# Layer 0's projections and router products in 32-column pieces, and the FFN's first weight tile moved by 224 bytes

## The chip, the cores and the metric

The kernel runs on one core of a Trainium2 chip. The metric is the device time of one execution in microseconds; of several runs the median is taken. A core has five engines that run side by side, each through its own instructions in order: TensorE (PE in the profile) multiplies, and its weight loads have a row of their own (PEld); VectorE (DVE), ScalarE (ACT) and GpSimd (POOL) work elementwise; SyncE (SP) issues most DMAs. Products land in PSUM, and everything else lies in SBUF, 128 partitions wide.

## The reference

Two transformer layers with post-norm on x of shape (8, 512, 512), all in float32:

```python
x = layernorm(x + attn0(x))   # 16 heads of 32, causal, with biases on Q, K, V and O
x = layernorm(x + moe(x))     # 8 experts, top 2, a router with a low-rank addition
x = layernorm(x + attn1(x))   # RMS-scaled input, 8 query heads of 64, 2 key heads
x = layernorm(x + ffn(x))     # gate, up and down from integers: (w - 128) * scale, width 1408
```

The router takes the softmax of the logits of each token, keeps the two largest, and divides them by their sum. An expert is silu(gate) * up and a down projection, with a low-rank addition to each weight.

## The kernel before

**Stages.** `usual_pass` runs four stages, one after the other on TensorE: attention of layer 0 with the routing (`attention0`, to about 712 us), the experts over tiles of 128 gathered tokens (`Tiles`), attention of layer 1 (`Attention1`, from about 1127 us), and the integer FFN (`IntegerFfn`, from about 1677 us). A batch is 512 tokens, held as four tiles of 128 rows; D = 512 is four chunks of 128. A float32 matmul of the program appears in the trace as two weight loads and two matmuls.

**A slot of layer 0.** For each batch b (8), each group g of four heads (4) and each unit u of key tiles (3), `attention0` issues one slot: `scores(b, g, u)` (L1386; keys of 32 rows, so four heads side by side in row groups of the array, 32\*128 in the profile), then the thunks that `plan(b)` put into this slot, then the `product` of the slot before (L1410; values of 32 columns, four heads side by side in column groups, 128\*32). Where a group ends, `normalise` follows (L1425, also 128\*32).

The thunks are the rest of the layer: `value`, `query` and `key` of this batch or the next (L1294, L1301, L1313), `project`, the output projection of the batch before (L1321), and the router two batches behind: `choose` (its gathers at L503 turn the four partial logits into eight per token), `dispatch` (ranks, L547 and L548), and `enter` (tables of tokens by expert, L588, in bf16). All these use the whole array, 128\*128. Others are `score` (logits, L491, 128\*32), `turn` (transposes, 128\*128) and `merge` (L781, 16 rows in a row group). In batches 1 to 6 each slot but the last of its twelve holds one or two projections.

Each projection is four products of 128 x 128 by 128 x 512, summed in one of two PSUM buffers (`p_mm`), and is taken out by VectorE (v, q, x) or ScalarE (k, and q of one group). The output projection of the last batch, the tables of the last two, and the gathers and ranks of the last run after the heads' buffers are closed, among the first expert tiles.

**What sets the order.** The framework orders each engine's instructions from dependences, the order of writing and its own estimate of durations. In the stretches under `in_order` (the first slot, and from the third group of the last batch on) TensorE follows the written order by force; in between the trace shows it in that order too. Other engines' orders are planned there.

**The FFN's weights.** `IntegerWeights` keeps the 33 units of 512 columns in two tiles. The first, `ffn_w0` of 20 units, is opened before layer 1's attention in the pool `c_weights` at the right end of SBUF; it holds the gate and up weights of hidden chunks 0 to 9. The second holds the down weights and chunk 10. `hidden` multiplies 128-column slices of them, as the stationary operand, with the two halves (high and low) of x (L1152 in the profile), 16 products a chunk; the down products (L1168) have the hidden tile as stationary operand and the weights as moving one.

**Layer 1** already makes most of its projections from two products of 64 columns each (`Attention1.multiply`, L1600).

Of the kernel before, what the change touches and what calls it, by code (L numbers as in the profile page):

```python
# [9 lines left out]
F32 = mybir.dt.float32  # L10
# [8 lines left out]
P = 128  # L19
# [3 lines left out]
NT = S // P  # L23
ND = D // P
E = 8
# [27 lines left out]

V_BQ, V_BK, V_NS, V_SS, V_SG, V_SU = 0, 4, 8, 12, 16, 16 + NHID
N_VEC = 16 + 2 * NHID


def in_order(tc, *engines):
# [358 lines left out]
class Router:  # L417
# [73 lines left out]
            self.nc.tensor.matmul(ps[32 * c : 32 * (c + 1), :], lhsT=self.wr[:, c, :], rhs=x1T[:, c, :],  # L491
                                  start=True, stop=True)

    def choose(self, b, parts, ps):

        nc, small = self.nc, self.small
        here = slice(NT * b, NT * (b + 1))

        def bc(a):
            return a[:, :, None].to_broadcast([P, NT, E])  # L500

        for t in range(NT):
            nc.tensor.matmul(ps[:, t, :], lhsT=parts[:, ts(t, P)], rhs=self.gather, start=True, stop=True)  # L503
        pr = small.tile([P, NT, E], F32, name="pr")
        tmp = small.tile([P, NT, E], F32, name="tmp")
        top = small.tile([P, NT], F32, name="top")
        second = small.tile([P, NT], F32, name="second")
        red = small.tile([P, NT], F32, name="red")
        total = small.tile([P, NT], F32, name="total")
        nc.vector.tensor_reduce(red, ps, AX.X, ALU.max)  # L510
        nc.vector.tensor_tensor(tmp, ps, bc(red), ALU.subtract)
        nc.scalar.activation(tmp, tmp, AF.Exp)
        nc.vector.tensor_reduce(red, tmp, AX.X, ALU.add)
        nc.vector.reciprocal(red, red)
        nc.vector.tensor_tensor(pr, tmp, bc(red), ALU.mult)

        def first_of_largest(values, largest, one_hot):
            nc.vector.tensor_reduce(largest, values, AX.X, ALU.max)
            nc.vector.tensor_tensor(tmp, values, bc(largest), ALU.is_equal)
            nc.vector.tensor_tensor(tmp, tmp, self.iota, ALU.mult)  # L520
            nc.vector.tensor_reduce(red, tmp, AX.X, ALU.min)
            nc.vector.tensor_tensor(one_hot, self.iota, bc(red), ALU.is_equal)

        first_of_largest(pr, top, self.hots[:, 0, here, :])

        rest = small.tile([P, NT, E], F32, name="rest")
        nc.vector.scalar_tensor_tensor(rest, self.hots[:, 0, here, :], -2.0, pr, ALU.mult, ALU.add)
        first_of_largest(rest, second, self.hots[:, 1, here, :])
        nc.vector.tensor_tensor(total, top, second, ALU.add)
        nc.vector.reciprocal(total, total)  # L530
        nc.vector.tensor_tensor(self.weights[:, 0, here], top, total, ALU.mult)
        nc.vector.tensor_tensor(self.weights[:, 1, here], second, total, ALU.mult)


        self.both = small.tile([P, NT, E], F32, name="both")
        nc.vector.tensor_tensor(self.both, self.hots[:, 0, here, :], self.hots[:, 1, here, :], ALU.add)
        self.earlier = small.tile([P, NT, E], F32, name="earlier")
        nc.vector.tensor_copy(self.earlier[:, 0, :], self.carry)
        for t in range(1, NT):
            nc.vector.tensor_tensor(self.earlier[:, t, :], self.earlier[:, t - 1, :], self.both[:, t - 1, :], ALU.add)  # L540
        nc.vector.tensor_tensor(self.carry, self.earlier[:, NT - 1, :], self.both[:, NT - 1, :], ALU.add)

    def dispatch(self, b, ps):

        nc, small = self.nc, self.small
        flat = "p t e -> p (t e)"
        nc.tensor.matmul(ps.rearrange(flat), lhsT=self.before, rhs=self.both.rearrange(flat), start=True, stop=False)  # L547
        nc.tensor.matmul(ps.rearrange(flat), lhsT=self.ones, rhs=self.earlier.rearrange(flat), start=False, stop=True)  # L548
        here = slice(NT * b, NT * (b + 1))
        parts = small.tile([P, TOP_K, NT], F32, name="parts")  # L550
        for k in range(TOP_K):
            for of_expert, out in ((ps, self.ranks[:, k, here]), (self.part, parts[:, k, :])):
                mine = small.tile([P, NT, E], F32, name="mine")
                nc.vector.tensor_tensor(mine, of_expert, self.hots[:, k, here, :], ALU.mult)
                nc.vector.tensor_reduce(out, mine, AX.X, ALU.add)

        rank = small.tile([P, TOP_K, NT], I32, name="rank")
        nc.vector.tensor_copy(rank, self.ranks[:, :, here])
        tile_of = small.tile([P, TOP_K, NT], I32, name="tile_of")
        nc.vector.tensor_scalar(tile_of, rank, 7, None, ALU.arith_shift_right)  # L560
        nc.vector.tensor_scalar(rank, rank, P - 1, None, ALU.bitwise_and)
        self.to_lane = small.tile([P, TOP_K, NT], F32, name="to_lane")
        nc.vector.tensor_copy(self.to_lane, rank)
        nc.vector.tensor_tensor(self.to_column[:, :, here], tile_of, parts, ALU.add)
# [15 lines left out]
                                    ALU.is_equal)  # L580
        return low, high, column

    def enter(self, ps, low, high, column):

        nc, n = self.nc, TOP_K * NT
        for h, part in enumerate((low, high)):
            for i in range(n):
                nc.tensor.matmul(ps[:, h, :], lhsT=part[:, i, :], rhs=column[:, i, :], start=i == 0, stop=i == n - 1)  # L588
        nc.vector.tensor_tensor(self.table, ps[:, 0, :], self.table, ALU.add)
        nc.vector.scalar_tensor_tensor(self.table, ps[:, 1, :], float(P), self.table, ALU.mult, ALU.add)  # L590

# [631 lines left out]
def attention0(env, guard, keep, routes, experts, dram, p_mm, tiles_ctx):  # L1223
# [8 lines left out]
    with ExitStack() as phase:  # L1232
# [55 lines left out]
        def mm(shape, name):  # L1288
            return p_mm.tile(shape, F32, tag="mm", name=name)

        def value(b, t):
            ps = mm([P, D], "ps_v")
            for c in range(ND):
                nc.tensor.matmul(ps, lhsT=xts[b][:, c, ts(t, P)], rhs=wv[:, c, :], start=c == 0, stop=c == ND - 1)  # L1294
            vs[t] = own.tile([P, D], F32, tag=f"v{t}", name=f"v{t}")
            nc.vector.tensor_tensor(vs[t], ps, row[:, 0, :], ALU.add)

        def query(b, g):
            ps = mm([P, S], "ps_q")
            for c in range(ND):  # L1300
                nc.tensor.matmul(ps, lhsT=wq[:, g, ts(c, P)], rhs=xts[b][:, c, :], start=c == 0, stop=c == ND - 1)  # L1301
            q = own.tile([P, S], F32, tag="q", name="q", bufs=2)
            if g == ND - 1 and 0 < b <= by_blocks:

# [5 lines left out]
        def key(b, g):  # L1310
            ps = mm([P, S], "ps_k")
            for c in range(ND):
                nc.tensor.matmul(ps, lhsT=wk[:, g, ts(c, P)], rhs=xts[b][:, c, :], start=c == 0, stop=c == ND - 1)  # L1313
            k = own.tile([P, S], F32, tag="k", name="k", bufs=2)
            nc.scalar.activation(k, ps, AF.Identity, bias=vec[:, V_BK + g : V_BK + g + 1])
            heads[b, g].append(k)

        def project(b, t):
            ps = mm([P, D], "ps_o")
            for c in range(ND):  # L1320
                nc.tensor.matmul(ps, lhsT=aoTs[b][:, c, ts(t, P)], rhs=wo[:, c, :], start=c == 0, stop=c == ND - 1)  # L1321
            nc.vector.tensor_tensor(xs[b][:, t, :], ps, xs[b][:, t, :], ALU.add)
            if t == NT - 1:
                env.layernorm(b, router.rows[S * b : S * (b + 1)])
# [34 lines left out]
            else:  # L1359
                nc.scalar.copy(logits[b], ps)  # L1360

        def choose(b):
            router.choose(b, logits.pop(b), mm([P, NT, E], "ps_r"))

        def dispatch(b, mm=mm):
            router.dispatch(b, mm([P, NT, E], "ps_rank"))

        rooms = {}

# [2 lines left out]
                rooms[b] = work.tile([P, ND, S], F32, tag="x1T", name="one_hot")  # L1372
            return router.one_hot(b, rooms[b], places)

        def enter(rows, mm=mm):
            router.enter(mm([P, 2, E * E_TILES], "ps_table"), *rows)

        def scores(b, g, u):
            q, k = heads[b, g]
# [162 lines left out]
        tiles.step(merge)  # L1542
        b = NB - 1
        one_hot(b - 1, (0, 1))
        project(b, 0)
        project(b, 1)
        rows = one_hot(b - 1, (2, 3))
        project(b, 2)
        project(b, 3)
        experts.load(7)  # L1550
        enter(rows)
        for _ in range(2):
            tiles.step()
            merge()
# [2 lines left out]
        tiles.step()  # L1557
        score(b)
        merge()
        choose(b)  # L1560
        tiles.step()
        merge()
        dispatch(b, tiles.aside)
        for places in ((0, 1), (2, 3)):
            rows = one_hot(b, places)
            tiles.step()
            merge()
        enter(rows, tiles.aside)
        tiles.of_fixed = router.fixed(routes)
        while merges:  # L1570
            tiles.step()
# [5 lines left out]
class Attention1:  # L1577
# [17 lines left out]
        return self.p_mm.tile(shape, F32, tag="mm", name=name)  # L1595

    def multiply(self, b, out, lhsT, rhs, c):

        for m in (slice(0, self.HD), slice(self.HD, P)) if b else (slice(0, P),):
            self.nc.tensor.matmul(out[m], lhsT=lhsT[:, m], rhs=rhs, start=c == 0, stop=c == ND - 1)  # L1600

    def prepare(self, b):

# [264 lines left out]
def usual_pass(tc, ins, held_out):  # L1868
    nc = tc.nc
    with ExitStack() as ctx:  # L1870
# [4 lines left out]
        with tc.tile_pool(name="a_mm", bufs=2, space=PSUM) as p_mm, ExitStack() as attn1_ctx:  # L1875
# [26 lines left out]
            for b in range(2, NB):  # L1902
                load_rows(b)
            weights = IntegerWeights(env, guard)
            weights.open(ctx.enter_context(tc.tile_pool(name="c_weights", bufs=1, side="right")), weights.FIRST)
            ffn = IntegerFfn(env, guard, weights, rows, dram)
            last_norm = attention.run(weights, ffn.split)
        ffn.run(held_out, last_norm)
# [306 lines left out]
```

## Time and profile before

| | |
|---|---|
| median of 3 runs | 2182.87 us (2181.64 to 2183.12) |
| the profiled execution: time | 2183.3 us |
| its span in the profile | 2181.6 us |
| TensorE busy, matmuls | 2151.6 us, 99% of the span, 9694 of them |
| V, Q, K, O projections of layer 0, busy | 116.3, 120.7, 117.5, 115.9 us |
| gathers, ranks, tables (all batches), busy | 7.7, 5.6, 15.3 us |
| FFN: gate and up, busy by four groups | 139.0, 138.8, 138.7, 138.6 us |

A row of the timeline gives a start, a length, engine, line, operation, the tile written and those read, rows\*columns of the array that the matmul uses, the moving operand's shape, and how many instructions were merged. Matmuls overlap:[...] lengths add up to more than the time taken, and the difference of two ends is the better measure. Busy time counts overlapping rows of a group once.

### The profile page before, as it was taken

The page shows a single profiled execution, that of the slowest core. Times are in us where ns is not written, and L with a number is a line of the kernel's source. Part 1 is how long each engine was busy: PE and PEld are TensorE (multiplying, and loading weights), DVE is VectorE, ACT ScalarE, POOL GpSimd, SP SyncE. Part 2 cuts the span into 40 slices and gives each one's busy share as a digit, 9 for nine tenths or more (in the row PEclk, how much of TensorE's full clock was granted, in tenths as well). Part 3 has the DMA queues.
Part 4 walks back from the last instruction along what each step waited for, and adds up shares of the span by engine and source line. Part 5 has one row for each costly group of instructions (what it writes and reads, how often), then busy time and mean ns, then how long its engine had stood idle before and what let it go on. Part 6 is the DMA issues. An engine that isn't in the chain of part 4 may idle for free. (4 is left out here: it accounts for less than half of the span.)

```text
span 2181.6 us, 25149 instructions
## 1 busy us (share of the span) xinstructions
PE 2151.6 (99%) x9694; PEld 1077.7 (49%) x9694; DVE 1273.8 (58%) x2042; ACT 627.5 (29%) x907; POOL 497.8 (23%) x489
## 2 busy tenths in 40 slices
PE   9999999999999999999999999999999999999997
PEld 3334444444444444444443333333334888888876
DVE  3557665675758543324316988889857644555443
ACT  2332323323223231122123333333332232222222
POOL 2332414324233442132015122231211000000000
PEclk9999999999999999999999999999999999999999
DMA  8030302303132328787644121331201311111000
GB/s 304 20 94 4 97 20 78 97 1 97 33 102 78 107 67 232 212 228 207 192 142 157 49 87 58 97 97 39 78 1 44 102 59 58 58 58 58 20 20 21
DMA packets 159971, 194.87 MB, mean 89 GB/s; under 512 B 61011, under 2 KB 101971, under 8 KB 157283
## 3 DMA queue, kind: packets, MB, share of 16 engines
q1 hardware_dynamic: 148560, 157.49, 23.5%
q0 software_dynamic: 10560, 34.61, 5.5%
q8 instruction: 79, 1.29, 0.2%
q10 hardware_dynamic: 722, 1.07, 0.1%
q14 instruction: 50, 0.40, 0.1%
HBM read 123.67 MB, written 69.47 MB: 89 GB/s over the span
## 5 line engine op out<-in xcount | busy, mean ns | idle before, releaser
L903 PE MATMUL ps_gu<-experts,xrT 128*128 128x512 f32 (+1 forms) x520 | 247.2, 598 | 0.0
L1390 ACT ACTIVATE p<-sc 128x2048 f32<-128x2048 f32 (+1 forms) x96 | 152.9, 1592 | 162.2 <-PE sc L1386 135.8
L1157 DVE SCALAR_TENSOR_TENSOR hT<-ps_u,vec,sg 128x512 f32<-128x512 f32 x88 | 65.6, 745 | 194.6 <-PE ps_u L1152 194.6
L1395 POOL TENSOR_SCALAR_AFFINE_SELECT p<-p 128x512 f32<-128x512 f32 x128 | 92.4, 734 | 360.3 <-ACT p L1390 316.8
L1168 PE MATMUL ps_f<-ffn_w,h_half 128*128 128x512 f32 x672 | 170.3, 393 | 0.6 <-issue 0.4
L1007 POOL TENSOR_TENSOR g_total<-g_total,r_inv 128x512 f32<-128x512 f32 x64 | 89.6, 1400 | 343.7 <-DVE r_inv L1778 272.2
L1418 DVE TENSOR_TENSOR p<-p 128x1536 f32<-128x1536 f32 (+2 forms) x96 | 131.1, 1365 | 46.0 <-POOL p L1395 41.0
L1748 ACT ACTIVATE p<-sc 128x1024 f32<-128x1024 f32 x128 | 124.0, 1021 | 100.4 <-PE sc L1745 95.9
L905 DVE TENSOR_TENSOR h<-ps_gu,h 128x256 f32<-128x256 f32 x67 | 28.4, 424 | 208.8 <-ACT h L904 208.8
L1778 DVE RECIPROCAL r_inv<-r_inv 128x512 f32<-128x512 f32 x32 | 107.1, 3346 | 69.3 <-ACT r_inv L1004 69.3
L1168 PEld LDWEIGHTS ps_f<-ffn_w,h_half 128*128 128x128 f32 x672 | 124.3, 188 | 33.1 <-DVE h_half L1163 5.6
L903 PEld LDWEIGHTS ps_gu<-experts,xrT 128*128 128x128 f32 x520 | 95.8, 196 | 89.3 <-issue 89.0
L1152 PE MATMUL ps_g<-x_high,ffn_w 128*128 128x512 f32 x352 | 138.8, 394 | 0.9 <-DVE x L1719 0.9
L1152 PE MATMUL ps_g<-x_low,ffn_w 128*128 128x512 f32 x352 | 139.0, 395 | 0.0
L1152 PE MATMUL ps_u<-x_low,ffn_w 128*128 128x512 f32 x352 | 138.7, 394 | 0.0
L1152 PE MATMUL ps_u<-x_high,ffn_w 128*128 128x512 f32 x352 | 138.6, 394 | 0.0
L919 PE MATMUL ps_y<-experts,hT 128*128 128x512 f32 (+1 forms) x272 | 128.0, 593 | 0.5 <-ACT hT L913 0.5
L1745 PE MATMUL sc<-qT,kT 64*128 64x512 f32 x512 | 127.2, 615 | 1.0 <-ACT qT L1653 0.7
L1301 PE MATMUL ps_q<-experts 128*128 128x512 f32 x256 | 120.7, 613 | 4.8 <-DMA experts<-in_xT 4.5
L1767 PE MATMUL av<-p,v 128*64 128x512 f32 x512 | 120.9, 593 | 0.0
L1313 PE MATMUL ps_k<-experts 128*128 128x512 f32 x256 | 117.5, 602 | 0.0
L1600 PE MATMUL ps_o<-attn_out,aoT 128*64 128x512 f32 x512 | 116.4, 598 | 0.8 <-ACT r_inv L1004 0.8
(267 smaller groups left out, 3359.6 us busy)
## 6 DMA issues: line engine op xcount, KB each, us to landing
results<-y SPq DMA_DIRECT2D x68, 256.0 KB, 2.2
turned<-turned SPq DMA_DIRECT2D x56, 256.0 KB, 4.1
pair<-xrT SPq DMA_DIRECT2D x25, 512.0 KB, 2.9
xrT<-pair SPq DMA_DIRECT2D x100, 128.0 KB, 4.3
x<-in_x SPq DMA_DIRECT2D x8, 1024.0 KB, 8.5
experts<-in_gate_up SPq DMA_DIRECT2D x8, 1024.0 KB, 11.0
rows<-x SPq DMA_DIRECT2D x32, 256.0 KB, 2.3
x<-rows SPq DMA_DIRECT2D x8, 1024.0 KB, 16.2
```

The lines of the kernel that those rows point to most:

```text
L903: nc.tensor.matmul(ps, lhsT=xT[:, c, :], rhs=self.weights(i, c), start=c == 0, stop=c == ND - 1)
L919: self.nc.tensor.matmul(ps, lhsT=hT[:, c, :], rhs=self.weights(i, ND + c), start=c == 0, stop=c == self.NI - 1)
L1152: nc.tensor.matmul(ps, lhsT=w[:, ts(dc, P)], rhs=x[:, dc, :], start=(dc, i) == (0, 0), stop=(dc, i) == (ND - 1, 1))
L1168: self.nc.tensor.matmul(os[t], lhsT=h[:, ts(t, P)], rhs=self.weights(2 * NHID + c), start=(c, i) == (0, 0), stop=(c, i) == (NHID - 1, 1))
L1301: nc.tensor.matmul(ps, lhsT=wq[:, g, ts(c, P)], rhs=xts[b][:, c, :], start=c == 0, stop=c == ND - 1)
L1313: nc.tensor.matmul(ps, lhsT=wk[:, g, ts(c, P)], rhs=xts[b][:, c, :], start=c == 0, stop=c == ND - 1)
L1390: nc.scalar.activation(p, sc[:, :, :width], AF.Exp, scale=scale)
L1418: nc.vector.tensor_tensor(total[:, :, P * kt :], total[:, :, P * kt :], p[:, :, at : at + w], ALU.add)
L1600: self.nc.tensor.matmul(out[m], lhsT=lhsT[:, m], rhs=rhs, start=c == 0, stop=c == ND - 1)
L1745: nc.tensor.matmul(sc[:, j, :], lhsT=st["kT"][hs, ts(kt, P)], rhs=st["qT"][g][hs, :], start=True, stop=True)
L1748: nc.scalar.activation(p, sc, AF.Exp, scale=scale)
L1767: nc.tensor.matmul(st["av"][HD * j : HD * (j + 1), :], lhsT=st["v"][:, kt, HD * j : HD * (j + 1)], rhs=p[:, j, :], start=kt == 0, stop=kt ...
```

## The change

A helper, `matmul_by_columns`, writes one product as several, each with 32 columns of the stationary operand into 32 partitions of the output. Layer 0's value, query, key and output projections use it, and so do the router's gathers, ranks and tables, as long as they run among the heads; after the heads' buffers are closed, the products keep their 128 columns (`out_of_heads`, `columns=P`). `Attention1.multiply` calls the helper with the widths that it had. Beside that, the pool of the FFN's first weight tile gets a second tile of 56 float32 (224 bytes) that nothing reads or writes.

```diff
+def matmul_by_columns(nc, out, lhsT, rhs, start=True, stop=True, columns=32):
+    for at in range(0, P, columns):
+        m = slice(at, at + columns)
+        nc.tensor.matmul(out[m], lhsT=lhsT[:, m], rhs=rhs, start=start, stop=stop)
...
-            nc.tensor.matmul(ps[:, t, :], lhsT=parts[:, ts(t, P)], rhs=self.gather, start=True, stop=True)
+            matmul_by_columns(nc, ps[:, t, :], parts[:, ts(t, P)], self.gather, columns=columns)
...
-        nc.tensor.matmul(ps.rearrange(flat), lhsT=self.before, rhs=self.both.rearrange(flat), start=True, stop=False)
-        nc.tensor.matmul(ps.rearrange(flat), lhsT=self.ones, rhs=self.earlier.rearrange(flat), start=False, stop=True)
+        out = ps.rearrange(flat)
+        matmul_by_columns(nc, out, self.before, self.both.rearrange(flat), stop=False, columns=columns)
+        matmul_by_columns(nc, out, self.ones, self.earlier.rearrange(flat), start=False, columns=columns)
...
-                nc.tensor.matmul(ps[:, h, :], lhsT=part[:, i, :], rhs=column[:, i, :], start=i == 0, stop=i == n - 1)
+                matmul_by_columns(nc, ps[:, h, :], part[:, i, :], column[:, i, :], i == 0, i == n - 1, columns)
...
+        def multiply(out, lhsT, rhs, c):
+            matmul_by_columns(nc, out, lhsT, rhs, start=c == 0, stop=c == ND - 1)
...
-                nc.tensor.matmul(ps, lhsT=wq[:, g, ts(c, P)], rhs=xts[b][:, c, :], start=c == 0, stop=c == ND - 1)
+                multiply(ps, wq[:, g, ts(c, P)], xts[b][:, c, :], c)
...
+        def wide(out, lhsT, rhs, c):
+            nc.tensor.matmul(out, lhsT=lhsT, rhs=rhs, start=c == 0, stop=c == ND - 1)
+
+        def project(b, t, out_of_heads=False):
...
+                (wide if out_of_heads else multiply)(ps, aoTs[b][:, c, ts(t, P)], wo[:, c, :], c)
...
-        def choose(b):
-            router.choose(b, logits.pop(b), mm([P, NT, E], "ps_r"))
+        def choose(b, columns=HD):
+            router.choose(b, logits.pop(b), mm([P, NT, E], "ps_r"), columns)
...
-        project(b, 0)
-        project(b, 1)
+        project(b, 0, True)
+        project(b, 1, True)
...
-        enter(rows)
+        enter(rows, columns=P)
...
-            weights.open(ctx.enter_context(tc.tile_pool(name="c_weights", bufs=1, side="right")), weights.FIRST)
+            pool = ctx.enter_context(tc.tile_pool(name="c_weights", bufs=1, side="right"))
+            weights.open(pool, weights.FIRST)
+            pool.tile([P, 56], F32, name="c_aligned")
```

`value` and `key` change as `query` does, and `dispatch` takes `columns` as `choose` does. `HD` is 32 in `attention0`, `P` is 128.

More of the change, by code (lines that the diff above doesn't have):

```diff
@@ L492, in logits, with choose @@
                                   start=True, stop=True)
-    def choose(self, b, parts, ps):
+    def choose(self, b, parts, ps, columns):
         nc, small = self.nc, self.small
@@ L541, in choose, with dispatch @@
         nc.vector.tensor_tensor(self.carry, self.earlier[:, NT - 1, :], self.both[:, NT - 1, :], ALU.add)
-    def dispatch(self, b, ps):
+    def dispatch(self, b, ps, columns):
         nc, small = self.nc, self.small
         flat = "p t e -> p (t e)"
-        nc.tensor.matmul(ps.rearrange(flat), lhsT=self.before, rhs=self.both.rearrange(flat), start=True, stop=False)
-        nc.tensor.matmul(ps.rearrange(flat), lhsT=self.ones, rhs=self.earlier.rearrange(flat), start=False, stop=True)
+        out = ps.rearrange(flat)
+        matmul_by_columns(nc, out, self.before, self.both.rearrange(flat), stop=False, columns=columns)
+        matmul_by_columns(nc, out, self.ones, self.earlier.rearrange(flat), start=False, columns=columns)
         here = slice(NT * b, NT * (b + 1))
@@ L581, in one_hot, with enter @@
         return low, high, column
-    def enter(self, ps, low, high, column):
+    def enter(self, ps, low, high, column, columns):
         nc, n = self.nc, TOP_K * NT
@@ L1293, in value @@
             for c in range(ND):
-                nc.tensor.matmul(ps, lhsT=xts[b][:, c, ts(t, P)], rhs=wv[:, c, :], start=c == 0, stop=c == ND - 1)
+                multiply(ps, xts[b][:, c, ts(t, P)], wv[:, c, :], c)
             vs[t] = own.tile([P, D], F32, tag=f"v{t}", name=f"v{t}")
@@ L1312, in key @@
             for c in range(ND):
-                nc.tensor.matmul(ps, lhsT=wk[:, g, ts(c, P)], rhs=xts[b][:, c, :], start=c == 0, stop=c == ND - 1)
+                multiply(ps, wk[:, g, ts(c, P)], xts[b][:, c, :], c)
             k = own.tile([P, S], F32, tag="k", name="k", bufs=2)
@@ L1316, in key @@
             heads[b, g].append(k)
-        def project(b, t):
+        def wide(out, lhsT, rhs, c):
+            nc.tensor.matmul(out, lhsT=lhsT, rhs=rhs, start=c == 0, stop=c == ND - 1)
+        def project(b, t, out_of_heads=False):
             ps = mm([P, D], "ps_o")
             for c in range(ND):
-                nc.tensor.matmul(ps, lhsT=aoTs[b][:, c, ts(t, P)], rhs=wo[:, c, :], start=c == 0, stop=c == ND - 1)
+                (wide if out_of_heads else multiply)(ps, aoTs[b][:, c, ts(t, P)], wo[:, c, :], c)
             nc.vector.tensor_tensor(xs[b][:, t, :], ps, xs[b][:, t, :], ALU.add)
@@ L1360, in score, with dispatch @@
                 nc.scalar.copy(logits[b], ps)
-        def choose(b):
-            router.choose(b, logits.pop(b), mm([P, NT, E], "ps_r"))
-        def dispatch(b, mm=mm):
-            router.dispatch(b, mm([P, NT, E], "ps_rank"))
+        def choose(b, columns=HD):
+            router.choose(b, logits.pop(b), mm([P, NT, E], "ps_r"), columns)
+        def dispatch(b, mm=mm, columns=HD):
+            router.dispatch(b, mm([P, NT, E], "ps_rank"), columns)
         rooms = {}
@@ L1373, in one_hot, with enter @@
             return router.one_hot(b, rooms[b], places)
-        def enter(rows, mm=mm):
-            router.enter(mm([P, 2, E * E_TILES], "ps_table"), *rows)
+        def enter(rows, mm=mm, columns=HD):
+            router.enter(mm([P, 2, E * E_TILES], "ps_table"), *rows, columns)
         def scores(b, g, u):
@@ L1544, in attention0 @@
         one_hot(b - 1, (0, 1))
-        project(b, 0)
-        project(b, 1)
+        project(b, 0, True)
+        project(b, 1, True)
         rows = one_hot(b - 1, (2, 3))
-        project(b, 2)
-        project(b, 3)
+        project(b, 2, True)
+        project(b, 3, True)
         experts.load(7)
-        enter(rows)
+        enter(rows, columns=P)
         for _ in range(2):
@@ L1559, in attention0 @@
         merge()
-        choose(b)
+        choose(b, P)
         tiles.step()
         merge()
-        dispatch(b, tiles.aside)
+        dispatch(b, tiles.aside, P)
         for places in ((0, 1), (2, 3)):
@@ L1567, in attention0 @@
             merge()
-        enter(rows, tiles.aside)
+        enter(rows, tiles.aside, P)
         tiles.of_fixed = router.fixed(routes)
@@ L1597, in multiply @@
     def multiply(self, b, out, lhsT, rhs, c):
-        for m in (slice(0, self.HD), slice(self.HD, P)) if b else (slice(0, P),):
-            self.nc.tensor.matmul(out[m], lhsT=lhsT[:, m], rhs=rhs, start=c == 0, stop=c == ND - 1)
+        matmul_by_columns(self.nc, out, lhsT, rhs, c == 0, c == ND - 1, self.HD if b else P)
     def prepare(self, b):
```

## The prediction

> **What bounds the kernel.** I read the page's first part, then busy time by stretch, then the waits of TensorE, then single stretches of the timeline.
>
> ```profile
> PE 2151.6 (99%) x9694; PEld 1077.7 (49%) x9694; DVE 1273.8 (58%) x2042; ACT 627.5 (29%) x907; POOL 497.8 (23%) x489
> core 0: us, PE busy (x) PEld busy (x) DVE busy (x) ACT busy (x) POOL busy (x), PEclk, DMA share, GB/s
> 14.00:697.00 683.00, 677.34 (x3526) 284.11 (x3530) 430.99 (x757) 213.44 (x232) 227.13 (x205) 1.00 0.24 76
> ...
> 1677.00:2170.00 493.00, 491.99 (x2114) 394.19 (x2114) 243.19 (x407) 130.49 (x205) 10.37 (x18) 1.00 0.16 53
> PE sc L1386 <- ACT p L1390: 2.0, 2, 1.8
> PE rs L1425 <- DVE first_h L905: 1.8, 1, 1.8
> PE ps_logits L491 <- ACT scaled L792: 1.7, 6, 0.3
> ```
>
> TensorE works through all four stages; the change touches the first (layer 0's attention, to 712 us) and the last (the integer FFN, from 1677 us). In the first it waits for others some 8 us from 14 us on, half of that after 690 us, in the last batch. So time that TensorE itself doesn't need is time gained, and the question is what TensorE's 677 us hold besides streaming.[...] One slot and a stretch of an earlier batch:
>
> ```profile
> 299.31 1.45 PE L1321 MATMUL ps_o<-experts,aoT 128*128 128x512 f32 x3
> 300.69 1.06 PE L1410 MATMUL av<-p,v 128*32 128x512 f32 x8
> 301.57 1.04 PE L1425 MATMUL rs<-p,ones 128*32 128x512 f32 x8
> 302.54 0.71 PE L1386 MATMUL sc<-q,k 32*128 32x256 f32 x8
> 303.19 3.70 PE L1313 MATMUL ps_k<-experts 128*128 128x512 f32 x8
> 306.72 3.60 PE L1321 MATMUL ps_o<-experts,aoT 128*128 128x512 f32 x8
> 310.16 1.91 PE L588 MATMUL ps_table<-one_hot 128*128 128x256 bf16 x16
> ...
> 55.14 1.14 PE L1386 MATMUL sc<-q,k 32*128 32x512 f32 x8
> 56.21 0.64 PE L1410 MATMUL av<-p,v 128*32 128x256 f32 x8
> ```
>
> A float32 product is two records. L1321's eight end 3.43 us after L1313's eight: 0.429 us a record. L1425's eight, four 32-column products side by side, end 0.86 us after L1410's: twice 0.429, so four narrow products cost what one 128-column product costs. The rest shows where the shape changes. L1313 ends at 306.89, 3.64 after L1386's end (303.25), 0.21 over eight times 0.429. L1410 at 300.69 ends 0.99 after L1321, 0.13 over 0.86. L1386 ends 0.64 after L1425, 0.21 over the 0.43 of two rows of 256. The last two lines are the change that the edit would leave: L1386 ends at 56.28, L1410 at 56.85, 0.57, which is 0.14 over 0.43.
>
> Over all single records from 14 to 712 us, by median, with the number of changes: rows (32\*128) to full (128\*128) 220 ns, 86; full to columns (128\*32) 121 ns, 78; rows to columns 120 ns, 18; columns to rows 215 ns, 91; full to rows 196 ns, 13; columns to full 220 ns, 5. Inside one shape the excess is 2 ns. (0.13 and 0.14 above hold 0.02 of stagger among four pieces.)
>
> In the FFN:
>
> ```profile
> 1911.05 0.39 PE L1152 MATMUL ps_g<-x_high,ffn_w 128*128 128x512 f32 x1
> ...
> 1914.77 1.98 PE L1168 MATMUL ps_f<-ffn_w,h_half 128*128 128x512 f32 x8
> 1916.59 0.39 PE L1152 MATMUL ps_g<-x_high,ffn_w 128*128 128x512 f32 x1
> ...
> 1920.21 1.98 PE L1168 MATMUL ps_f<-ffn_w,h_half 128*128 128x512 f32 x8
> ```
>
> These are hidden chunks 9 and 10 of a batch, 16 products each: 3.72 us and 3.62 us. By single records, products whose stationary operand lies in the first weight tile (chunks 0 to 9) start 233.2 ns apart in the mean, all others in the stage (chunk 10 from the second tile, and the down products, whose stationary operand is the hidden tile) 226.7. The program's addresses: the first tile begins at byte 138720 of a partition, 32 past a multiple of 64; the second at 92416, a multiple of 256; the hidden tiles are multiples of 256 too.
>
> [...] no run here shows a narrow bf16 load. [...] on entering a shape, the second float32 load starts 107 ns after the first at 128 columns and 27 ns after four staggered ones at 32. [...] the 6.5 ns rest on the trace alone.
>
> **The change part by part.** (1) *Projections.* V, Q, K of eight batches and the output projection of seven are 3 x 128 + 112 = 496 products; each becomes four pieces. Streaming: 858 ns before and after, by L1425 against L1321; layer 1 does the same with 64 columns at 429 ns a pair (L1600). Cost nothing, gain nothing.
>
> (2) *Shape changes.* With V, Q, K, in-loop O, gathers, ranks and tables as columns, I relabel TensorE's recorded sequence and count again: rows to full 86 to 4, full to columns 78 to 4, rows to columns 18 to 100, columns to rows 91 to 102, full to rows 13 to 2, columns to full 5 to 3. Times the medians: -18.0 - 9.0 + 9.8 + 2.4 - 2.2 - 0.4 = **-17.4 us**. What stays full: transposes, the first expert products, the count.
>
> Does anything hide it? In four slots of the first batch and one of each later one the scores come soon after k (L1315): k was finished 205 ns before the scores' load, and where that wait does bind (14.71 us) it is 53 ns, so 150 ns are spare and the edit takes 120. The exponential (L1390) ends at least 0.47 us before the next scores, and in slots that hold a projection 1.7 us or more, but for the last batch. The x1T round trip by DMA has 25 us. The L491 and last-batch waits above stay as they are. Next late after this would be k, by 30 ns.
>
> (3) *Small products.* Gathers: 7 batches, 4 products of 8 columns; ranks: 7 times 2; tables: 6 times 16 in bf16, 1.75 us each now (109 ns a record). Each becomes four pieces with a quarter of the load, and L1410's 128-column rows step at 109 ns for four pieces, as the full ones do. So the estimate is nothing; below nothing is excluded, since both are at 107 ns of loading. Above: the densest long run in the trace is layer 1's V, 128 records in 3.44 us, 27 ns a record. If that were the issue limit, tables cost 128 x 27 = 3.5 us (+1.7 x 6), gathers 1.7 (+0.86 x 7), ranks 0.86 (+0.43 x 7): +19 us. Against it: where TensorE's sequencer came out of a wait with nothing queued (1147.61 us), two products, eight records, were loaded with 36 ns between them, 9 ns a record, under the 13.6 needed. I take **+1.0 us** for the bf16 loads and for waits in the last batch.
>
> (4) *Pad.* The pool lies at the right end and grows down; its first tile has the lowest address (as r_ones lies under r_before in the same kind of pool). So the tile moves by 224 bytes to 138496, a multiple of 256, with the same remainder as the second tile up to 1024. 8 batches x 10 chunks x 16 products x 6.5 ns = **-8.4 us**. The stage waits 1.6 us in its first batch and 0.3 to 0.5 us in the others; VectorE has 243 of 493 us, so nothing takes it back. The DVE's conversions write the moved tile in layer 1 off the path. Bounds: 0 (it isn't the address) to -8.4.
>
> (5) *Nothing elsewhere.* No DMA is added or moved; instruction records grow by 3516 loads and as many matmuls[...].
>
> Sum: -17.4 + 1.0 - 8.4 = -24.8. The profiled execution's span is 2181.6 and its time 2183.3; these become 2156.8 and 2158.5. The median of the runs, 2182.87, becomes **2158**.
>
> **Rivals.** *The pad does nothing* (10%): the slow loads have to do with that region or with who wrote it, not with the 32 bytes. Only two tiles stand behind the address reading. 2166.5.
>
> *The switches come back as waits* (13%): outside the last batch VectorE's order is planned by the framework from its own estimate of durations, and four pieces may look four times as long to it. An evacuation put behind a reciprocal (3.35 us, L1428) then holds one of two PSUM buffers. For it: VectorE is busy 431 of 683 us there and its order differs from the written one today. Against it: TensorE is in the written order and no such wait shows now. Losing half to all of 17.4: 2167 to 2175.
>
> *Slower: issue of instructions* (7%). A product grows from 4 records in 858 ns to 16, 54 ns each. If TensorE can't take records that fast for long, streaming stops hiding it. The place is L1294 to L1321, runs of one to three products; it decides at 54 ns a record[...]. Against it: 27 ns over 128 records, and 9 ns after a wait.
>
> *Neither part shows* (2%): 2180 to 2184.
>
> **How the numbers follow.** The forecast has 68%, with its own range 2154 to 2162: the throttle's half-clock periods (the granted clock is 0.99 in the expert stage) can come or go at 1 to 2 us each. The range for 8 in 10 takes in the pad's failure and the milder lost waits: 2153 to 2170. Faster by over 0.2% (about what a measurement of this kernel can tell from no change) is 68 + 10 + 13 = 91%, less 1 for the tail of lost waits; same 3%; slower 7%.
>
> **What would show it.** Right: no row 32\*128 followed by 128\*128 except at transposes and first expert rows; L1294 and its like in pieces 128\*32, 858 ns a product; the stretch to the first expert rows 16 to 17 us shorter; L588's successor 1.75 us a table; chunks 0 to 9 of the FFN at 226.7 ns, the stage 8 us shorter. Wrong: pieces further apart than 429 ns a group, new waits of TensorE on DVE v, q or x, tables of 2.3 us or more, or 233 ns left in the FFN.

## The result and the profile after

The changed kernel takes **2160.95 us** (median of 5 runs, 2159.8 to 2162.94); before takes 2182.47 (5 runs, 2181.64 to 2183.12). The ratio is **0.9902**, 95% interval 0.9888 to 0.9917: some 21.5 us faster. The profiled execution has a span of 2159.1 us where before has 2181.6.

The first part of the page after, and busy time in the two stretches that answer to those shown of before:

```profile
PE 2125.0 (98%) x13210; PEld 1017.5 (47%) x13210; DVE 1278.6 (59%) x2042; ACT 627.4 (29%) x907; POOL 499.2 (23%) x489
core 0: us, PE busy (x) PEld busy (x) DVE busy (x) ACT busy (x) POOL busy (x), PEclk, DMA share, GB/s
14.00:697.00 683.00, 672.51 (x7082) 229.99 (x7078) 451.91 (x794) 219.75 (x241) 232.84 (x211) 1.00 0.25 77
1661.00:2148.00 487.00, 483.86 (x2114) 394.72 (x2114) 243.31 (x409) 130.45 (x205) 10.71 (x18) 1.00 0.17 54
```

TensorE has the 3516 records more that were forecast (9694 to 13210), and is no longer busy all the time: in 683 us of layer 0 some 10 us are idle, where before it was under 6. In the FFN it now has 3 us without work, where before it had one. The waits of TensorE (total, times, longest) say on whom:

```profile
PE sc L1400 <- ACT p L1404: 2.4, 1, 2.4
PE rs L1439 <- DVE first_h L913: 2.0, 1, 2.0
PE ps_f L1176 <- DVE h_half L1171: 1.9, 7, 0.5
PE ps_x1T L1361 <- DVE g_routed L605: 1.5, 1, 1.5
...
PE ps_o L62 <- DVE q L1318: 0.7, 1, 0.7
```

The third was 0.2 us before, the fourth under 0.2, and the last wasn't there. A slot of layer 0, from the timeline of TensorE (all column products now have the helper's line, L62):

```profile
295.44 0.71 PE L1400 MATMUL sc<-q,k 32*128 32x256 f32 x8
296.08 3.64 PE L62 MATMUL ps_k<-experts 128*32 128x512 f32 x32
299.54 3.62 PE L62 MATMUL ps_o<-experts,aoT 128*32 128x512 f32 x32
302.98 1.93 PE L62 MATMUL ps_table<-one_hot 128*32 128x256 bf16 x64
304.72 1.05 PE L1424 MATMUL av<-p,v 128*32 128x384 f32 x16
```

L62's k ends 3.57 us after the scores, where it was 3.64. The table's 64 records end 1.75 us after the output projection between them (at 303.16), as before; and av follows with no change of shape.

Where the 22.5 us of span went, from the starts of the same products in both traces: 0.9 before the first scores (TensorE's steps of 512 columns fall from 0.85 us to 0.43 after some 7.3 us of the span, in the kernel before after some 9.2; the pieces of Q and K there step at 0.43 a group, as the full products do), **14.1** from there to the last batch of layer 0, 0.2 in the last batch, nothing in the expert stage, 1.0 in layer 1 (where a wait of 1.1 us of the row sums for VectorE's `total` is gone; no run here shows why), **6.2** in the FFN.

### The profile page after: what moved, and what is told of

Its sections match the earlier page's. It is cut to its first block, busy times and chain, and to the rows that moved or that the text cites. A ratio compares the mean times of both kernels' runs of the same rounds, so it can differ in the third digit from the quotient of the medians.

```text
span 2159.1 us, 32188 instructions
## 1 busy us (share of the span) xinstructions
PE 2125.0 (98%) x13210; PEld 1017.5 (47%) x13210; DVE 1278.6 (59%) x2042; ACT 627.4 (29%) x907; POOL 499.2 (23%) x489
## 3 DMA queue, kind: packets, MB, share of 16 engines
q8 instruction: 107, 1.75, 0.3%
q10 hardware_dynamic: 722, 1.07, 0.1%
## 5 line engine op out<-in xcount | busy, mean ns | idle before, releaser
L1432 DVE TENSOR_TENSOR p<-p 128x1536 f32<-128x1536 f32 (+2 forms) x96 | 138.8, 1446 | 44.3 <-POOL p L1409 41.1
L62 PE MATMUL ps_q<-experts 128*32 128x512 f32 x1024 | 120.6, 600 | 5.0 <-DMA experts<-in_xT 4.6
L62 PE MATMUL ps_o<-attn_out,aoT 128*64 128x512 f32 x512 | 116.4, 598 | 0.8 <-ACT r_inv L1012 0.8
L62 PE MATMUL ps_k<-experts 128*32 128x512 f32 x1024 | 116.3, 594 | 0.0
```

The costliest lines, as they stand in the source:

```text
L62: nc.tensor.matmul(out[m], lhsT=lhsT[:, m], rhs=rhs, start=start, stop=stop)
L1432: nc.vector.tensor_tensor(total[:, :, P * kt :], total[:, :, P * kt :], p[:, :, at : at + w], ALU.add)
```

## The experiments

All are compared with before; medians are of 4 to 10 runs if nothing else is said. "To the last batch" is the stretch from the first scores to the first scores of batch 7; it repeated within 0.7 us between executions of kernels with the same layer 0. The last batch itself didn't: in two profiled executions of the changed kernel it took 85.6 and 88.4 us to the first expert rows, since a half-clock period fell ahead of those rows in one (granted clock 0.66 from 680 to 690 us, with the period in part of it) and behind them in the other (1.00 there, 0.50 from 697 to 703 us). The kernel before has two such periods, of 3.4 us at 0.50 each, from 712 and 764 us. So the last batch is left out of fine comparisons.

### One part alone

Pad alone (before, with the pad):

```diff
+            pool.tile([P, 56], F32, name="c_aligned")
```

> Pad alone, layer 0 as before. Theory (the address of the stationary tile sets the pace, and the FFN's VectorE then becomes late at each batch boundary): chunks 0 to 9 at 226.7 ns a product, the seven waits on h_half there as in the changed kernel (1.9 us), the FFN stage 486.4 us instead of 492.6, its start unmoved at 1677; time 6.2 us below before. Rival A (the forecast's step 4, nothing takes it back): stage 484.2, 8.4 below. Rival B (the pad does nothing): 492.6 and no difference.

Measured: 2176.9 us, ratio 0.9973 (0.9964 to 0.9983), 5.8 below the 2182.72 of before beside it. The FFN takes 486.46 us, its start is not earlier, the seven waits on h_half are there (1.9 us). Chunks 0 to 9 stand 226.8 ns apart against 233.0. So the pad's effect is its own, and so are the waits. The theory holds, both rivals fall.

Columns alone (the changed kernel, that line removed):

> All products of layer 0 as in the changed kernel, without the pad. Theory (the two parts don't touch each other): the FFN starts at 1661 (16 us earlier than before), its stage takes 492.6 us with chunks 0 to 9 at 233.2 ns; time 16 us below before. Rival (moving layer 0 alone costs or saves something in the FFN, such as another half-clock period): the stage is off 492.6 by more than 0.5 us.

Measured: 2167.27 us, ratio 0.9932 (0.9918 to 0.9946), 15.5 below before; the FFN starts at 1661.3 and takes 492.59 us. The parts are independent: 5.8 and 15.5 make 21.3.

### Small products and projections apart

Projections full again, small products by columns:

```diff
-            matmul_by_columns(nc, out, lhsT, rhs, start=c == 0, stop=c == ND - 1)
+            nc.tensor.matmul(out, lhsT=lhsT, rhs=rhs, start=c == 0, stop=c == ND - 1)
```

> Changed kernel with the pad, but projections full as before: only gathers, ranks and tables are columns. The number of changes of shape is then that of before. Theory (narrow loads into different column groups overlap): gathers 0.4 us and ranks 0.1 us shorter a batch, tables unchanged, 3.8 us before the FFN, and with the pad's 6.2 a time 10 us below before. Rival (forecast's step 3: nothing gained): the FFN starts where it started before, time 6.2 below. Rival (the 0.5 us a batch came from a change of shape that fell away): also 6.2 below.

Measured: 2173.4 us, ratio 0.9962 (0.9948 to 0.9975), 9.3 below before and 3.5 below the pad alone; to the last batch 4.2 us less than before. The other way round:

```diff
-        def choose(b, columns=HD):
+        def choose(b, columns=P):
...
-        def dispatch(b, mm=mm, columns=HD):
+        def dispatch(b, mm=mm, columns=P):
...
-        def enter(rows, mm=mm, columns=HD):
+        def enter(rows, mm=mm, columns=P):
```

> Changed kernel, but gathers, ranks and tables are full again, among projections by columns. Theory (a full product among column products now pays a change of shape in and one out, and narrow gathers and ranks are faster in themselves): 20 places x (0.22 + 0.12) = 6.8 us of changes, and 3.8 us of small products: 10.6 us above the changed kernel. Rival (the forecast's step 3: narrow small products gain nothing in themselves): 6.8 above.[...]

Measured: 2168.45 us, ratio 0.9937 (0.9923 to 0.9951), some 7 above the changed kernel. The gathers show both effects. TensorE's timeline from V over the gathers to av, in the kernel before, with small products alone as columns, with projections alone, and in the changed kernel:

```profile
354.29 2.31 PE L1294 MATMUL ps_v<-experts 128*128 128x512 f32 x5
356.44 0.95 PE L503 MATMUL ps_r<-r_gather,logits 128*128 128x8 f32 x8
357.32 0.64 PE L1410 MATMUL av<-p,v 128*32 128x256 f32 x8
```

```profile
347.61 7.13 PE L1300 MATMUL ps_v<-experts 128*128 128x512 f32 x16
354.68 0.44 PE L62 MATMUL ps_r<-r_gather,logits 128*32 128x8 f32 x32
354.95 0.64 PE L1424 MATMUL av<-p,v 128*32 128x256 f32 x8
```

```profile
345.38 7.07 PE L62 MATMUL ps_v<-experts 128*32 128x512 f32 x64
352.38 1.06 PE L62 MATMUL ps_r<-r_gather,logits 128*128 128x8 f32 x8
353.37 0.64 PE L1424 MATMUL av<-p,v 128*32 128x256 f32 x8
```

```profile
346.45 2.76 PE L62 MATMUL ps_v<-experts 128*32 128x512 f32 x24
349.03 0.44 PE L62 MATMUL ps_r<-r_gather,logits 128*32 128x8 f32 x31
...
349.32 0.65 PE L1424 MATMUL av<-p,v 128*32 128x256 f32 x7
```

From V's end to av's end it is 1.36, 0.85, 1.56 and 0.76 us. (In the changed kernel one record of the gathers comes after the first of av, among the lines left out.) In the second kernel the number of shape changes is that of before (V is full, av is columns), and 0.51 us are gone all the same: the narrow gathers are faster in themselves. In the third there are two changes more than in the changed kernel. The same sum over a whole undisturbed batch (batch 5; from single records, the time by which each group's last end lies behind all ends before it, us):

| | before | changed | small products alone | projections alone | 64 columns |
|---|---|---|---|---|---|
| V, Q, K, O | 57.1 | 56.4 | 57.1 | 56.4 | 56.6 |
| av | 10.13 | 8.82 | 9.76 | 9.17 | 10.13 |
| gathers and ranks | 1.16 | 0.38 | 0.63 | 1.55 | 0.62 |
| tables | 1.75 | 1.75 | 1.86 | 1.85 | 1.75 |
| the rest | 19.2 | 19.4 | 19.2 | 19.2 | 19.2 |
| batch | 89.34 | 86.76 | 88.56 | 88.26 | 88.30 |

Small products alone gain 0.78, projections alone 1.08, both together 2.57: the remaining 0.7 exist only together, because full small products among column projections pay a change in and one out. The narrow loads overlap: in the changed kernel the loads of these gathers, 110 ns each, mostly start 7 to 12 ns apart, where the full ones of 190 ns start 111 ns apart. Of my expectations, 3.8 us for small products alone was right to within half a microsecond (3.5 between the two kernels with a pad). The 10.6 us for projections alone were 7: over 20 places the direct sum is 10.5, but the slower kernel has some 4 us less of waits (the scores wait 1.6 us for p, x1T 0.3 for g_routed and V not at all for scaled, against 2.4, 1.5 and 1.1 in the changed kernel).

### Is it the shape or the narrowness?

Pieces of 64 columns for everything that the change converts, av and rs staying at 32:

```diff
-            matmul_by_columns(nc, out, lhsT, rhs, start=c == 0, stop=c == ND - 1)
+            matmul_by_columns(nc, out, lhsT, rhs, start=c == 0, stop=c == ND - 1, columns=64)
```

and 64 for HD in the three defaults above.

> Changed kernel with pieces of 64 columns in layer 0 instead of 32; its neighbours stay at 32. Theory (the tile's shape must be the same): some 80 places go from 64 to 32 columns, each up to 0.12 us: up to 9.7 us above the changed kernel, and V, Q, K, O themselves at 858 ns a product as before. Rival A (only going between row tiles and column tiles is paid): within 1 us of the changed kernel. Rival B (64 columns count as full): a row to 64 columns costs 0.22 instead of 0.14 as well, some 17 above.

Measured: 2171.08 us, ratio 0.9946 (0.9933 to 0.996), some 10 above the changed kernel; to the last batch 9.6 more. From 64 to 32 columns costs 127 ns (median of 76), as much as from full to 32 (120), and rows to 64 costs 166 against 140 to 32. So here leaving 64 columns for 32 costs what leaving 128 does: half the width is no half step.

### How near is the limit of issue?

V in four quarters of 128 moving columns, 64 records a product instead of 16 (one run):

```diff
-            for c in range(ND):
-                multiply(ps, xts[b][:, c, ts(t, P)], wv[:, c, :], c)
+            for n in range(NT):
+                for c in range(ND):
+                    multiply(ps[:, ts(n, P)], xts[b][:, c, ts(t, P)], wv[:, c, ts(n, P)], c)
```

> Changed kernel, but each narrow piece of V is done in four quarters of 128 moving columns: 64 records a product in place of 16, 13.4 ns each if streaming still sets the pace. Theory (no limit of issue near 54 ns a record, the slower rival falls with room to spare): V at 858 ns a product, or somewhat above, where the limit shows as a time per record. Slower rival at 27 ns a record: 1716 ns a product, 128 products, 110 us above the changed kernel; at 54 ns: 330 above.

Measured: 2173.32 us, 12 above the changed kernel. Its timeline, the first two V of batch 0 and then of a later batch:

```profile
15.75 4.35 PE L62 MATMUL ps_v<-experts 128*32 128x128 f32 x150
22.04 3.24 PE L62 MATMUL ps_v<-experts 128*32 128x128 f32 x106 [1.94 <-issue]
...
353.57 7.19 PE L62 MATMUL ps_v<-experts 128*32 128x128 f32 x256
```

In the later batch eight products end 7.2 us after the scores (most other such pairs 7.1) where it is 7.0 in the changed kernel: 512 records (loads and matmuls) at 14 ns each, where eight products at 858 ns make 6.9 us, so streaming still sets the pace. Batch 0 alone takes 78.5 us instead of 68.2. Two waits for issue make 6.5 us of that. A half-clock period from 29.6 to 36.4 us, which the changed kernel doesn't have there (its granted clock is 1.00 from 14 to 300 us; the mean of the whole span is 0.995 with V in quarters and 0.996 without), makes some 2.6 more (an estimate: V goes on at 31.25 us, and at the 0.50 of the periods above half of the 5.2 us to the period's end is lost). So the slower rival is refuted with a factor of nearly four to spare in a steady stretch. At the program's start the same density of records did make TensorE wait for issue, though even so the first two V take 9.5 us, 19 ns a record. Why issue is slow there wasn't tried. In the changed kernel the DMA share is 1.05 to 1.07 from 14 to 40 us, and TensorE has no wait for issue there.

### What in the pad matters

Pads of 32, 96 and 64 bytes instead of 224 (4 runs of the first, one of each other):

```diff
-            pool.tile([P, 56], F32, name="c_aligned")
+            pool.tile([P, 8], F32, name="c_aligned")
```

> Changed kernel with a pad of 32 bytes instead of 224: the first weight tile begins at byte 138688, a multiple of 64 but not of 128. Theory A (a multiple of 64 is enough): chunks 0 to 9 at 226.7 ns, no difference to the changed kernel. Theory B (a wider alignment is needed): 233.2 ns, the FFN stage 492.6 us, 6 us above the changed kernel.

and, in the same line, 24 and 16 in place of 8:

> Pad of 96 bytes: the first weight tile begins at byte 138624, a multiple of 128 but not of 256. So far: 233.0 ns a product at 32 bytes past a multiple of 64, 229.3 at a multiple of 64, 226.7 at a multiple of 256. Theory A (128 is enough): chunks 0 to 9 at 226.7. Theory B (each step of alignment gives its part): between 226.7 and 229.3. Theory C (what counts is 256): 229.3.

> Pad of 64 bytes: the first weight tile begins at byte 138656, 32 past a multiple of 64 as before, only elsewhere. Theory (the remainder to 64 sets the pace): 233 ns a product in chunks 0 to 9. Rival (it is the place of the tile, or the pad's mere presence): 226.7 to 229.3.

What each pad gives (mean interval of chunks 0 to 9; totals 2164.89, ratio 0.9922, 0.9907 to 0.9937, then 2170.43 and 2169.49):

| pad, bytes | first tile at | past a multiple of 256 | ns a product |
|---|---|---|---|
| 0 | 138720 | 224 | 233.0 |
| 32 | 138688 | 192 | 229.3 |
| 64 | 138656 | 160 | 233.2 |
| 96 | 138624 | 128 | 232.5 |
| 224 | 138496 | 0 | 226.8 |

So it is the address, but neither of the simple rules: a multiple of 64 isn't enough, and the multiple of 128 is worse than the odd multiple of 64, which no theory of mine expected. The stationary tiles that run at full speed (138496, 92416 and the hidden tiles from 63744 on) lie 256 past a multiple of 1024, and so do the moving ones (37120, 45312, 71936 and 80128); whether the remainder itself counts or the distance to the moving tile was not tried and stays open. Nor does the pace go with the product's own tile alone. In the kernel before, the last down product ahead of such a chunk also ends 233.4 ns behind the one before it, and the last product of the chunk ahead of down products only 228.7. With pads of 96 and 64 bytes the down products, of whose tiles none moved, step more slowly too (229.6 and 230.3 ns in the mean, against 228.5 before and 227.6 in the changed kernel; steps over 300 ns, which hold waits, are left out). With these pads the stage takes 493.4 and 494.5 us, more than before's 492.6 (one execution each).

### Getting back what was lost

In the FFN the layernorm of a batch is called in the next batch's second chunk:

```diff
-            env.layernorm(b, env.ins.out[b])
...
+            if c == 1 and b:
+                env.layernorm(b - 1, env.ins.out[b - 1])
```

> Changed kernel, but in the FFN the layernorm of a batch is called two chunks later, so that VectorE's nine instructions of statistics and its wait for POOL's rstd no longer stand ahead of the next batch's first hidden tile. Theory (that queue is what made h_half late): the waits on h_half (1.9 us) go, the FFN stage takes 484.5 us instead of 486.4. Rival (the 5 us of y and x adds ahead of it are enough to make it late, or another wait comes): 486.4 stays.

Measured: 2158.61 us, ratio 0.9892 (0.9877 to 0.9907). The stage takes 482.3 us (4.1 less, twice what was expected), and no wait on h_half is left. The time is only 2.3 us below the changed kernel's; in the profiled execution the last batch of layer 0 took 1.6 us longer than there, with a half-clock period in it. The timeline of the changed kernel at a batch boundary shows why it was late:

```profile
1793.35 1.92 DVE L192 TENSOR_SCALAR x<-x,mv,rstd 128x512 f32<-128x512 f32 x4 [0.84 <-POOL rstd L190]
...
1795.18 1.29 DVE L1171 TENSOR_TENSOR h_half<-hT,h_half 128x512 fp32r<-128x512 f32 x2
...
1795.92 0.51 PE L1176 MATMUL ps_f<-ffn_w,h_half 128*128 128x512 f32 x1 [0.26 <-DVE h_half L1171]
```

VectorE waits 0.84 us for POOL's rstd with the next batch's halves queued behind it. The view of waits counted 1.9 us; by the ends of the down products the seven boundaries cost 3.9 (0.49 to 0.76 each), since after a wait the load of the late tile's weights (0.19 us) is exposed too: at this boundary the view counts 0.26 us, and the first down product then ends 0.51 us after its load began, where the next ones take 0.40. They cost 1.8 in the kernel before, 0.2 to 0.5 each: the stall was there, small, before the pad.

On top of that, in layer 0's last batch the router's choice one slot later:

```diff
-                    todo[2, 2].append(lambda: choose(pb))
+                    todo[3, 0].append(lambda: choose(pb))
```

> The kernel with the later layernorm, and in layer 0's last batch the router's choice of the batch before one slot later, so that its small exponential stands behind the slot's large one on ScalarE instead of ahead of it. Theory (the 2.4 us in which the scores wait for p are due to this order for about 1 us): that wait falls to 1.4 us, the rest as in the kernel with the later layernorm, about 1 us less. Rival (VectorE's chain is the one that is late, and the choice now delays it further): the waits on first_h or g_routed grow by as much.

and the changed kernel itself, beside it:

> The changed kernel itself, to stand beside the version with later layernorm and choice on one chip. Theory: 2161, the other some 4 to 5 below, as far as no half-clock period falls differently. Rival (the FFN's gain is lost elsewhere): both within 1 us.

Measured: **2157.51 us** (2155.66 to 2159.37), ratio 0.9886 (0.9869 to 0.9902), against 2161.57 (2160.82 to 2162.46), ratio 0.9902 (0.9885 to 0.9918): 4.1 us faster than the changed kernel. The FFN's 4.0 us account for all of it. The choice's move gained nothing that shows; the waits of this kernel:

```profile
PE ps_xrT L886 <- DVE first_turned L887: 2.6, 1, 2.6
...
PE sc L1400 <- ACT p L1404: 1.2, 1, 1.2
```

The scores' wait fell from 2.4 to 1.2 as expected, and the transposes of the first expert rows wait 2.3 us longer: the rival's case, VectorE being the late one there, on another tile than it named.

## Why the prediction was right, and where its steps were off

**The time.** 2158 was forecast, 2160.95 came; it lies in the range for 8 in 10 and in the likeliest case's own range. The two main causes, changes of shape and the tile's address, were right. That the sum came so near is partly luck: errors of several microseconds stood against each other inside it.

**Step 1, projections cost nothing.** Right: 0.429 us a group of four pieces, 3.43 to 3.44 per four products, before and after.

**Step 2, shape changes, -17.4.** The counts came out as relabelled (rows to columns 100, columns to rows 101, rows to full 2). Leaving a full shape for columns was worth a little more than was said: in nine places of batch 5 av ends 0.137 us earlier (1.00 to 0.86 or 0.57 to 0.43), not 0.121, some 1.2 us over 74 places. Entering was overpriced. The 120 ns for rows to columns were the median of 18 changes, and 13 of these follow single products of 16 rows, those of `merge` above all. The other five, from the four scores side by side, already cost 140 in the trace of before (counted, as the 220 are, from the first of the four), and this is the kind that the edit makes: 140 in the trace after too, with 256 or 512 moving columns. And the last of four staggered pieces ends 0.02 later than a full product would. So V, Q, K and O gained 0.06 us a place (3.63 to 3.57), not 0.10: about 3.4 us less over 86 places.

**A term that the sum didn't have: batch 0.** It takes 68.2 us before and after, so its 2.2 us never came. Its Q is interleaved with scores by the planner, not by the written order, before as well as after: that TensorE keeps the written order throughout, as is said ahead of the prediction and in it, doesn't hold there. TensorE's timeline there, before and then after:

```profile
56.78 1.98 PE L1301 MATMUL ps_q<-experts 128*128 128x512 f32 x4
58.70 1.15 PE L1386 MATMUL sc<-q,k 32*128 32x384 f32 x16
59.77 1.98 PE L1301 MATMUL ps_q<-experts 128*128 128x512 f32 x4
```

```profile
55.56 1.88 PE L62 MATMUL ps_q<-experts 128*32 128x512 f32 x10
57.37 1.15 PE L1400 MATMUL sc<-q,k 32*128 32x384 f32 x16
58.45 2.77 PE L62 MATMUL ps_q<-experts 128*32 128x512 f32 x22
```

Before, the scores stand between the second and the third product; after, between the fifth and the sixth *piece*. The second product is torn into one piece and three, and streams nearly twice: the one ends 0.84 us after the piece before it and the three 0.85, where the four pieces of a product take 0.86 together. Q's products of batch 0 take 1.7 us longer, in three places. That the torn products eat the gain is read from the traces; a kernel that keeps them together wasn't run.

**Step 3, small products, +1.0.** Wrong in sign. "Below nothing is excluded, since both are at 107 ns of loading" failed: narrow loads into different column groups overlap. A gather's narrow load takes 110 ns, not a quarter of the full one's 190, but the next starts 7 to 12 ns after it. I had read the rows of 128 moving columns, which step at 109 ns by streaming, as if loading held them. Small products alone gain 0.78 us a batch, some 5 us in all by direct sums. The tables were priced right (1.75 us): their narrow bf16 loads take 97 ns each and start 7 ns apart in fours, where the full ones take 98 ns. The +1.0 us set aside for these loads and for waits was my estimate; no narrow bf16 load is in the trace of before.

**The last batch.** Forecast -2 with a microsecond of waits; it kept its length, but for 0.2 us. What was saved on TensorE turned into waits, for g_routed (1.5 us, under 0.2 before), q (0.7, none before), p (2.4, 1.8 before) and, a little later, first_h (2.0, 1.8 before): there VectorE and ScalarE are the late ones. In part that is the rival "the switches come back as waits", and the wait for q is the sign that the prediction named for it: an output projection needs the PSUM buffer that VectorE hasn't emptied. But VectorE is held there by the one_hot instructions of the router (639.8 to 645.3 us, then q to 645.99, and the output projection starts at 646.04), not by a reciprocal, and half of the scores' 2.4 us went when the router's choice was moved. Earlier, in batch 4, V waits 1.1 us for scaled (0.3 before).

**Step 4, pad, -8.4.** The interval was right: 1280 products at 6.2 ns by ends, -8.0. "Nothing takes it back" failed: the boundary steps grew from 1.8 to 3.9 us, and the stage gained 6.2. The argument was an average (VectorE busy half of the stage); at a boundary VectorE is busy for 11.2 of 12 us (1784 to 1796), and the rest is its wait for rstd. The reading "the address" was right (pad alone), the rule behind it, 32 past a multiple of 64, was not: 138624 is a multiple of 128 and slow. Nor were all other products of the stage at 226.7, as the reading had it: the last down product ahead of a slow chunk is slow too.

**The sum.** On one side 3.4 us of entry, batch 0's 2.2, the last batch's 1.8, the pad's 2.2 and 0.8 of waiting in batch 4 were missing. On the other stood small products (5 us gained, +1.0 forecast), 1.2 from leaving, and 1.9 in layer 1 and ahead of the first scores that no step named. The slower rival (issue at 54 ns a record or more) is refuted by the traces and by records at 14 ns.

## What to carry to other kernels

On TensorE, give neighbours the same tile shape down to the column count: a change cost 0.12 to 0.22 us here, by its direction, and cutting a full product into column pieces cost nothing (0.86 us a product before and after) as long as the pieces of one product stayed together (that tearing them costs is read from three places in one batch). Where a planner orders instructions, look at whether it tears such groups, and at what the other engines do just where TensorE gets faster: here one layernorm call moved gave 4 us, two thirds of what the pad itself had. If equal products run at two speeds (here 226.8 and 233.0 ns), compare the addresses of their stationary tiles, and try the new address rather than trust a rule of alignment.

## What the hardware showed that was not expected

- Stationary tiles of the same products at different addresses run at 226.7, 229.3, 232.5 or 233 ns, and not in the order of their alignment; at some addresses the products beside them, whose tiles didn't move, are slower too (229.6 and 230.3 ns against 227.6).
- Gathers of 8 moving columns: eight full records took 0.79 us, 32 narrow ones 0.37 with the change of shape included (0.99 for full ones with theirs).
- From 64 to 32 columns TensorE pays 127 ns, about as from 128 to 32 (120).
- 512 records in 7.2 us are no burden in the middle of the program (14 ns a record), but in its first batch TensorE waited 6.5 us for issue (one run).
